# Loading the image with its channels on the partitions, one column at a time, in place of transposes on TensorE

## The chip, the cores and the metric

The kernel runs on one core of a Trainium2 chip. The metric is the device time of one execution in microseconds (us). The kernel before was run three times: median 3004.53 us, from 3003.02 to 3005.59. Everything read from a profile comes from one further execution, recorded by the hardware profiler.

Engine names are those of the profile: PE is TensorE (matmuls), PEld its weight loads, DVE is VectorE, ACT is ScalarE, POOL is GpSimd. SP only starts transfers and waits for events; SPq and ACTq stand for DMA issues on the queues of SP and ACT.

## The reference

The input x has the shape 4 x 64 x 64 x 64: four elements of the batch, each an image of 64 rows (h) by 64 columns (w) with 64 channels (c), in fp32. Four attention layers follow each other, and the elements do not depend on each other. Of the first layer, which the change feeds, the reference computes this:

```python
b, h, w, c = x.shape
n = h * w                                            # 4096 tokens
q = (einsum('bhwc,cf->bhwf', x, Wq) + bq).reshape(b, n, c)
k = (einsum('bhwc,cf->bhwf', x, Wk) + bk).reshape(b, n, c)
v = (einsum('bhwc,cf->bhwf', x, Wv) + bv).reshape(b, n, c)
attn = softmax(einsum('bic,bjc->bij', q, k), axis=-1)   # 4096 x 4096 per element
out = einsum('bmn,bmc->bnc', attn, v)
x = gamma * out.reshape(b, h, w, c) + x
```

The kernel calls the four layers layer0 to layer3. Layer1 is a smaller attention, of 4096 queries by 1024 pooled keys. Layer2 and layer3 are again full 4096 x 4096 attentions, each with a group normalisation in front. So three layers have 4096 x 4096 scores for each of the four elements, and these scores and the sums with v make up nearly all of the work.

## The kernel before, in words

**Layout.** Most of the time an element's image lies in SBUF as a tile xT of 128 partitions by 2048 fp32 values: the 64 channels of the left half of the image (columns 0 to 31) on partitions 0 to 63, those of the right half (columns 32 to 63) on partitions 64 to 127, and along a partition the tokens of that half in the order row, column (h times 32 plus w). The matmuls of all layers read this layout, since the channels are what they sum over. In memory the image has its channels innermost, so xT is the transpose of what a plain load gives.

**How xT comes about.** `load_x` (L645) starts eight transfers of 128 KB on the SP queue (L653) into a tile xin that has tokens on the partitions and runs of 64 channels, 256 bytes each, along them. `transposed` (L909) then makes two groups of eight transposes of 128 x 128 on TensorE (L916) into a PSUM tile, and copies each group to half of xT (`evacuate`, L858: on VectorE at L862 for element 1, on ScalarE at L870 for elements 2 and 3; for element 0 on both). `before0` (L919) calls it, then `project` (L874, matmuls at L883) for the queries q, then `swapped` (L889, two transfers on SP at L893, which exchange the halves of q), then `values` (L896, matmuls at L902).

**Steps.** The program is written in steps (`step`, L808). In a step of layer0 (L949), layer2 or layer3 (`attention`, L1184) two blocks of scores are made (128 x 1024; matmuls L971 or L1199, exponentials L975 or L1204), and two earlier blocks are multiplied with v (L996 or L1234). A phase is 64 steps, and there are twelve: layer0 of elements 0 and 1, layer2 of element 0, layer0 of element 2, layer2 of element 1, and so on. All other work is background: a chain of generators handed to `background` (L777), which is advanced one piece at a time inside the steps (`advance`, L798) at a tempo given for the phase. A piece ends at each `yield`. What is left of the chain at the end of a phase is emitted at once (`drain`, L786). A function can also be tied to the start of a given step through the dictionary `before` (L773).

The order in which this program emits instructions is the order on each engine. It does not tie the engines to each other: an engine waits only for the data and the buffers that its next instruction needs. The queue of SP takes its transfers in the order in which they were emitted.

**Where the load and the transposes stand.** In the first phase (steps 0 to 63, layer0 of element 0) the background at tempo 1 ends with: the constants of the later layers, the load of element 1 (emitted in step 28), six pauses, `before0` of element 1 (transposes in steps 35 and 36, `project` in steps 37 and 38, `values` in steps 39 and 40), and the load of element 2 (step 41). Element 2's transposes run in the third phase (layer2 of element 0). Element 3 is loaded at the end of the background of the fourth phase, and transposed in the fifth.

**Buffers.** xin, xT, q, k, v and other tiles of 128 x 2048 come from one pool of 13 buffers (L626, `x_tile`, L631). A tile takes a buffer when it is first written, and gives it back after its last use.

**Other transfers on SP.** Between the loads stand the exchanges of halves: q_swapped and k_swapped (L893) and pg (L1059, in layer1), and at the end the output. In the compiled program a transfer also waits for the one that stands eight transfers earlier, since eight completion counters are handed round.

Of the kernel before, what the change touches and what calls it, by code (L numbers as in the profile page):

```python
# [597 lines left out]
def fast_path(tc: tile.TileContext, a: dict, out: bass.AP, bad):  # L598
# [9 lines left out]
    nc = tc.nc  # L608
    x = a["x"]
    B, H, W, C = x.shape  # L610
    N = H * W
    P = 128
    W2 = W // 2
# [6 lines left out]
    MID, ALONE, LATE, END = range(4)  # L620
# [10 lines left out]
    x_tile = lambda name: x_p.tile([P, S], FP, tag="x", name=name)  # L631
    p_tile = lambda: p_p.tile([P, 1024], FP, tag="p", name="p")
    o_tile = lambda name: o_p.tile([P, 512], FP, tag=name, name=name)
    half = lambda i: slice(i * C, (i + 1) * C)
# [6 lines left out]
    def tokens(ap):  # L641

        return ap.rearrange("(k r) (i w) c -> r w k i c", r=4, i=2)

    def load_x(st, parts=((slice(None), lambda r, i: nc.sync.dma_start),)):  # L645
        if "xin" not in st:
            st["xin"] = x_tile("xin").rearrange("p (k i c) -> p k i c", i=2, c=C)
        t = st["xin"]
        src = tokens(x[st["b"]])
        for ks, queue in parts:  # L650
            for r in range(4):
                for i in range(2):
                    queue(r, i)(t[r * W2 : (r + 1) * W2, ks, i, :], src[r, :, ks, i, :])  # L653

    def ctile(shape, name):
        return const.tile(shape, FP, tag=name, name=name)
# [3 lines left out]
    def column(name, src, reps=2):  # L660
        t = ctile([P, 1], name)
        n = P // reps
        for i in range(reps):
            load[0](t[i * n : (i + 1) * n, :], src.rearrange("(c o) -> c o", o=1))
        return t
# [106 lines left out]
    now = [0]  # L772
    due, before, urgent = {}, {}, []  # L773
# [3 lines left out]
    def background(tempo, *phases):  # L777
        def pieces():
            for ph in phases:
                yield from ph  # L780

        assert back["at"] is None
        back.update(gen=pieces(), credit=0.0, tempo=tempo)
        back["at"] = next(back["gen"], None)
# [64 lines left out]
    def banks(on):  # L849

        if on == "both" and now[0] < 2:
            bank = [acc_tile(), acc_tile()]
            return bank, bank
        s = s_tile()
        bank = [s[:, chunk(i)] for i in range(2)]
        return bank if on == "both" else s, bank

    def evacuate(on, dst, src, bias=None):  # L858

        if on == "DVE":  # L860
            if bias is None:
                nc.vector.tensor_copy(dst, src)  # L862
            else:
                nc.vector.tensor_scalar(dst, src, bias, None, ALU.add)
        elif on == "both":
            m = dst.shape[-1] // 2
            evacuate("DVE", dst[:, 0:m], src[0], bias)
            evacuate("ACT", dst[:, m:], src[1], bias)
        elif bias is None:
            nc.scalar.copy(dst, src)  # L870
        else:
            nc.scalar.activation(dst, src, AF.Identity, bias=bias)
# [16 lines left out]
    def swapped(name, t):  # L889

        o = x_tile(name)
        for i in range(2):
            nc.sync.dma_start(o[half(i), :], t[half(1 - i), :])  # L893
        return o
# [14 lines left out]
    def transposed(on, st):  # L909
        xin = st.pop("xin")  # L910
        xT = st["x"] = x_tile("xT")
        for g in range(2):
            yield MID
            s, bank = banks(on)
            for i in range(8):
                nc.tensor.transpose(bank[i // 4][:, ds(i % 4 * P, P)], xin[:, g * 8 + i, :, :].rearrange("p i c -> p (i c)"), ident)  # L916
            evacuate(on, xT[:, wide(g)], s)

    def before0(on, st):  # L919
        yield from transposed(on, st)  # L920
        q = x_tile("q")
        yield from project(on, q, blocks[0][0], st["x"], blocks[0][1])
        st["q"] = q, swapped("q_swapped", q)
        st["v"] = x_tile("v").rearrange("p (j f) -> p j f", f=C)
        yield from values(st["v"], wv0, st["x"], bv0)
# [16 lines left out]
    def second_half(st, v):  # L942
        yield from values(v, wv0, st["x"], bv0)
        for g in st.pop("todo"):
            yield MID
            for _ in g:
                pass

    def layer0(st):  # L949

        q, k, v = st.pop("q"), st["x"], st.pop("v")
        pairs = NB * NC // 2
        acc, ps, zs, scaled = {}, {}, {}, {}
        zsum, rz = check_columns(NB)

        def queries(m, i, e):

            c, n = divmod(m // 2, 4)
            return q[(c + i) % 2][half(i), ds(c // 2 * 1024 + m % 2 * 512 + n * P + e * C, C)]

        def first(u):
            m, c = divmod(u, NC)
            if c == 0:
                zs[m] = small.tile([P, NC], FP, tag="z0", name="z0")
            s = s_tile()
            for i in range(2):
                for e in range(2):  # L970
                    nc.tensor.matmul(  # L971
                        s[half(e), chunk(i)], queries(m, i, e), k[half(i), chunk(c)], start=True, stop=True
                    )
            p = ps[u] = p_tile()
            nc.scalar.activation(p, s, AF.Exp, accum_out=zs[m][:, c : c + 1])  # L975
            if c == NC - 1:
                nc.vector.tensor_reduce(zsum[:, m : m + 1], zs.pop(m), AX.X, ALU.add)  # L977
                nc.vector.reciprocal(rz[:, m : m + 1], zsum[:, m : m + 1])

        def scale(t):  # L980
            vs = scaled[t] = z_p.tile([P, C], FP, tag="vs", name="vs", bufs=1)
            for e in range(2):
                if 0 <= t - e < pairs:
                    m = 2 * (t - e) // NC
                    nc.scalar.activation(  # L985
                        vs[half(e), :], v[half(e), m, :], AF.Copy, scale=rz[half(e), m : m + 1]
                    )

        def add(t, e, n, vs, cols):

            if 0 <= t < pairs:
                m, c = divmod(2 * t + n, NC)
                if m == 0 and e == 0 and c not in acc:
                    acc[c] = acc_tile()
                for i in range(2):
                    nc.tensor.matmul(  # L996
                        acc[c][half(i), cols], vs[half(e), :], ps[2 * t + n][half(e), chunk(i)][:, cols],
                        start=(m == 0 and e == 0), stop=(m == NB - 1 and e == 1),
                    )
                    yield  # L1000

        def adds(t, n, within=None):
            for cols in parts(within, t * 2 < NC or t >= pairs - NC // 2):
                lower, upper = add(t, 0, n, scaled[t], cols), add(t - 1, 1, n, scaled[t], cols)
                for row_tile in (lower, upper) * 3:
                    next(row_tile, None)
            if n == 1:
                del scaled[t]
                for u in (2 * t - 2, 2 * t - 1):
                    ps.pop(u, None)  # L1010

        def finish(cs):
            xT = st["x"]
            for c in cs:
                nc.vector.scalar_tensor_tensor(xT[:, chunk(c)], acc.pop(c), gamma0, xT[:, chunk(c)], ALU.mult, ALU.add)
            if not acc:
                st["done0"] = True

        start = now[0]
        for t in range(pairs + 1):  # L1020
            g = start + t + 3
            before.setdefault(g, []).append(lambda t=t: scale(t))
            due.setdefault(g, []).extend([lambda *within, t=t, n=n: adds(t, n, *within) for n in range(2)])
        for g, cs in ((2, (0, 1)), (3, (2, 3))):
            due[start + pairs + g].append(lambda cs=cs: finish(cs))
        for t in range(pairs):
            step(lambda: (first(2 * t), first(2 * t + 1)))
        return start + pairs + 4
# [483 lines left out]
    s0, s1, s2, s3 = state  # L1512
    def rest(phase):
        yield MID
        yield from phase
# [7 lines left out]
    st0 = transposed("both", s0)  # L1523
# [70 lines left out]
    for n, dsts in spectra:  # L1594
        w_d, u_d = a["L1_conv_w_" + n], a["L1_conv_u_" + n]
        r, d = w_d.shape
        w, u = scratch2[:, at : at + d], scratch2[:, at + d : at + 2 * d]
# [100 lines left out]
    def pause(n):  # L1698
        yield from [MID] * n

    def loads(st):
        yield MID
        load_x(st)


    background(1.0, rest(st0), second_half(s0, s0["v"]), pause(6), constants(), loads(s1), pause(6), before0("DVE", s1), loads(s2))
    layer0(s0)
    drain()
    background(3.0, layer1("DVE", s0, False), before2("DVE", s0))
    free = layer0(s1)  # L1710
    drain()
    background(3.0, layer1("ACT", s1, True), before0("ACT", s2))
    free = layer2(s0, free)
    drain()
    background(1.0, before2("DVE", s1), loads(s3))
    free = layer0(s2)
    drain()
    background(3.0, layer1("ACT", s2, True), before0("ACT", s3))
# [99 lines left out]
```

## Time and profile before

| What | Value |
|---|---|
| median of three runs | 3004.53 us (3003.02 to 3005.59) |
| the profiled execution's own time | 3005.78 us |
| its span, first to last instruction | 3003.7 us |
| granted TensorE clock, mean | 0.999 |
| PE busy | 2979.2 us |
| ACT busy | 1943.8 us |
| DVE busy | 1760.1 us |
| DMA queue of SP: packets, MB, share of 16 engines | 40080, 21.17 MB, 3.7% |
| transposes of elements 1 to 3 (L916) | 48, median 273 ns one by one |
| their evacuations on VectorE (L862) | 2 of 1.23 us |
| loads of x, 128 KB each: median from issue to landing | 5.0 us |

How to read it: the span is the profiled execution from its first to its last instruction; its own time has 2.1 us more around it. An engine's busy time is the time in which it executed something. Matmuls overlap each other, so eight transposes of 273 ns took 1.09 us together. A DMA packet is what one of the 16 DMA engines moves for one descriptor, a contiguous run of bytes; the share of 16 engines is the time that all packets took, over 16 times the stretch looked at. In the listings of groups and of the timeline, a line begins with its start and duration in us, then engine, source line, operation, output<-input, shapes and count.

### The profile page before, as it was taken

To read this page: it belongs to the slowest core of one execution; us is meant where nothing else is said; L and a number is where in the kernel's file an instruction comes from. 1 tells how busy PE (TensorE), PEld (TensorE's weight loads), DVE (VectorE), ACT (ScalarE), POOL (GpSimd) and SP (SyncE) were. 2 spreads that over 40 slices of the span, in tenths; PEclk is the share of its full clock that TensorE was granted. 3 is DMA by queue.
4 is the path that set the end of the run, shared out by engine and by line. 5 is a ranking of instruction groups with operands and counts; after the bars stand their busy time and mean duration, and the time that the engine had idled before them with its cause. 6 is when DMAs were issued, how large, how long until landed. Compare 5 with 4: busy or idle time off the path is not lost.

```text
span 3003.7 us, 64700 instructions
## 1 busy us (share of the span) xinstructions
PE 2979.2 (99%) x28509; PEld 1133.0 (38%) x28509; DVE 1760.1 (59%) x2003; ACT 1943.8 (65%) x2816; POOL 34.1 (1%) x32
## 2 busy tenths in 40 slices
PE   9999999999999999999999999999999999999998
PEld 4333233433444433344443333333343334333333
DVE  1211332587731068772017887777887777877777
ACT  6877778666588866557886655655555655555554
POOL 0000000000000000000000000000000000000000
PEclk9999999999999999999999999999999999999999
DMA  2010000000001000000000000000000000000000
GB/s 37 2 29 5 1 1 2 19 2 1 15 1 29 1 5 1 15 2 10 7 2 5 2 8 9 19 5 8 5 19 6 17 1 1 12 12 5 9 5 9
DMA packets 42081, 25.79 MB, mean 9 GB/s; under 512 B 39872, under 2 KB 39872, under 8 KB 40384
## 3 DMA queue, kind: packets, MB, share of 16 engines
q1 hardware_dynamic: 40080, 21.17, 3.7%
q8 instruction: 225, 3.69, 0.5%
q10 hardware_dynamic: 1712, 0.41, 0.1%
q14 instruction: 64, 0.52, 0.1%
HBM read 4.79 MB, written 4.19 MB: 3 GB/s over the span
## 4 chain that ended last, share of the span: by engine, by line
PE 98%; ACT 1%; SPq 0%; DVE 0%; issue 0%; DMA 0%; ACTq 0%; DVEq 0%
PE acc L1234 30%; PE s L1199 30%; PE acc L996 15%; PE s L971 14%; PE s L1079 2%; PE acc L1105 1%; ACT p L1085 1%; PE s L883 1%; PE s L1105 1%; PE s L1262 1%; PE s L1346 0%; PE s L902 0%; PE s L1260 0%; PE s L1443 0%; PE s L1366 0%; PE s L1051 0%
## 5 line engine op out<-in xcount | busy, mean ns | idle before, releaser
L1204 ACT ACTIVATE p<-s 128x1024 f32<-128x1024 f32 x1024 | 994.8, 1022 | 705.6 <-PE s L1199 694.0
L1210 DVE TENSOR_TENSOR zacc<-zacc,p 128x1024 f32<-128x1024 f32 x960 | 1174.1, 1223 | 372.2 <-ACT p L1204 334.4
L975 ACT ACTIVATE p<-s 128x1024 f32<-128x1024 f32 x512 | 519.9, 1016 | 42.7 <-PE s L971 24.3
L1234 PE MATMUL acc<-p,v 64*64 64x512 f32 (+1 forms) x4456 | 525.2, 558 | 0.0
L996 PE MATMUL acc<-p,vs 64*64 64x512 f32 (+1 forms) x4224 | 512.2, 578 | 0.5 <-ACT vs L985 0.5
L1199 PE MATMUL s<-q,k 64*64 64x512 f32 x2048 | 495.5, 593 | 2.1 <-ACT p L1085 2.1
L1234 PE MATMUL acc<-p,hT 64*64 64x512 f32 x4096 | 494.1, 590 | 0.0
L971 PE MATMUL s<-xT,q 64*64 64x512 f32 x2048 | 487.4, 591 | 2.5 <-DVE v L903 0.6
L971 PE MATMUL s<-xT,q_swapped 64*64 64x512 f32 x2048 | 488.4, 591 | 0.0
L1199 PE MATMUL s<-q,xT 64*64 64x512 f32 x2048 | 486.9, 589 | 0.0
L1199 PE MATMUL s<-q,h_swapped 64*64 64x512 f32 x2048 | 479.4, 589 | 0.0
L1199 PE MATMUL s<-q,k_swapped 64*64 64x512 f32 x2048 | 477.6, 593 | 0.0
L977 DVE TENSOR_REDUCE all_z<-z 128x1 f32<-128x4 f32 x128 | 20.1, 157 | 643.2 <-ACT p L975 643.2
L1234 PEld LDWEIGHTS acc<-p,v 64*64 64x64 f32 x4456 | 179.9, 133 | 285.0 <-issue 280.0
L996 PEld LDWEIGHTS acc<-p,vs 64*64 64x64 f32 x4224 | 176.3, 133 | 270.3 <-issue 206.5
L985 ACT ACTIVATE vs<-v,all_r 64x64 f32<-64x64 f32 x512 | 177.2, 346 | 145.2 <-PE acc L996 72.4
L1234 PEld LDWEIGHTS acc<-p,hT 64*64 64x64 f32 x4096 | 156.7, 133 | 263.8 <-issue 263.1
L971 PEld LDWEIGHTS s<-xT,q_swapped 64*64 64x64 f32 x2048 | 145.8, 133 | 146.3 <-issue 114.2
L1199 PEld LDWEIGHTS s<-q,h_swapped 64*64 64x64 f32 x2048 | 143.9, 133 | 141.2 <-issue 135.5
L971 PEld LDWEIGHTS s<-xT,q 64*64 64x64 f32 x2048 | 145.8, 133 | 134.1 <-issue 106.0
L1199 PEld LDWEIGHTS s<-q,xT 64*64 64x64 f32 x2048 | 143.4, 133 | 140.1 <-issue 137.7
L1199 PEld LDWEIGHTS s<-q,k 64*64 64x64 f32 x2048 | 140.1, 132 | 148.3 <-issue 100.2
(233 smaller groups left out, 1560.2 us busy)
## 6 DMA issues: line engine op xcount, KB each, us to landing
k_swapped<-k SPq DMA_DIRECT2D x8, 512.0 KB, 6.0
h_swapped<-xT SPq DMA_DIRECT2D x8, 512.0 KB, 5.3
out_dram<-turned SPq DMA_DIRECT2D x62, 64.0 KB, 1.9
xin<-in_x_dram SPq DMA_DIRECT2D x24, 128.0 KB, 5.0
q_swapped<-q SPq DMA_DIRECT2D x6, 512.0 KB, 5.4
pg<-pg SPq DMA_DIRECT2D x8, 128.0 KB, 2.3
xin<-in_x_dram SPq DMA_DIRECT2D x12, 64.0 KB, 2.3
xin<-in_x_dram ACTq DMA_DIRECT2D x4, 64.0 KB, 2.6
```

The source lines that it names most:

```text
L883: nc.tensor.matmul(bank[i][half(e), :], w[half(i), half(e)], rhs[half(i), chunk(2 * j + (1 - e if exchanged else e))], start=True, stop=True,)
L971: nc.tensor.matmul(s[half(e), chunk(i)], queries(m, i, e), k[half(i), chunk(c)], start=True, stop=True)
L975: nc.scalar.activation(p, s, AF.Exp, accum_out=zs[m][:, c : c + 1])
L985: nc.scalar.activation(vs[half(e), :], v[half(e), m, :], AF.Copy, scale=rz[half(e), m : m + 1])
L996: nc.tensor.matmul(acc[c][half(i), cols], vs[half(e), :], ps[2 * t + n][half(e), chunk(i)][:, cols], start=(m == 0 and e == 0), stop=(m == ...
L1079: nc.tensor.matmul(ss[e][half(m), chunk(i)], pgs[0 if e == d else 1][r, ds(n * P + m * C, C)], th[r, chunk(2 * j + i)], start=True, stop=True,
L1085: nc.scalar.activation(pk[e], ss[e], AF.Exp)
L1105: nc.tensor.matmul(acc[quarter(q), :], g[:, k, :], ps[j, k][q // 2][:, chunk(q % 2)], start=(k == 0 or not bank), stop=(k == NK - 1 or not ...
L1199: nc.tensor.matmul(s[half(e), chunk(i)], k[(j + i) % 2][half(i), ds(j // 2 * P + e * C, C)], q[half(i), chunk(c)], start=True, stop=True,)
L1204: nc.scalar.activation(p, s, AF.Exp)
L1210: add = lambda: nc.vector.tensor_tensor(zaccs[c], p0, p, ALU.add)
L1234: nc.tensor.matmul(accs[c][e][half(i), cols], v[half(e), j, :], p[half(e), chunk(i)][:, cols], start=(j == 0), stop=(j == NB - 1),)
```

## The change

Elements 1, 2 and 3 are no longer loaded into xin and transposed. A new function, `load_transposed`, writes xT straight from memory: for each of the 64 image columns (half i, column w within the half) one transfer on SP, whose destination is 64 partitions (channels) by 64 rows with a step of 32 values, and whose source is the same elements in memory, where neighbouring channels are 4 bytes apart and neighbouring rows 16 KB. Neither side has a run of more than one fp32 value along its last dimension, so each transfer is made of 4096 descriptors of 4 bytes. Element 0 keeps the load and the transposes.

The 64 transfers of an element are tied to the starts of steps: for element 1 two in each step from step 6 of the first phase on, for elements 2 and 3 one in each step of the second and of the fourth phase. `before0` takes the finished tile and begins with `project`. In the first phase the chain loses the two loads and has fourteen pauses between the constants and `before0`. The generator `loads` goes away.

```diff
+    def load_transposed(st, first, rate):
+
+        xT = st["x"] = []
+        src = x[st["b"]].rearrange("h (i w) c -> i w c h", i=2)
+
+        def column(n):
+            if n == 0:
+                xT.append(x_tile("xT"))
+            i, w = divmod(n, W2)
+            dst = xT[0][half(i), :].rearrange("c (h w) -> w c h", w=W2)
+            nc.sync.dma_start(dst[w], src[i, w])
+
+        for n in range(W):
+            before.setdefault(now[0] + first + n // rate, []).append(lambda n=n: column(n))
+
     def before0(on, st):
-        yield from transposed(on, st)
+        (st["x"],) = st["x"]
         q = x_tile("q")
...
-    def loads(st):
-        yield MID
-        load_x(st)
-
-
-    background(1.0, rest(st0), second_half(s0, s0["v"]), pause(6), constants(), loads(s1), pause(6), before0("DVE", s1), loads(s2))
+
+    background(1.0, rest(st0), second_half(s0, s0["v"]), pause(6), constants(), pause(14), before0("DVE", s1))
+    load_transposed(s1, 6, 2)
     layer0(s0)
     drain()
     background(3.0, layer1("DVE", s0, False), before2("DVE", s0))
+    load_transposed(s2, 0, 1)
     free = layer0(s1)
     drain()
     background(3.0, layer1("ACT", s1, True), before0("ACT", s2))
     free = layer2(s0, free)
     drain()
-    background(1.0, before2("DVE", s1), loads(s3))
+    background(1.0, before2("DVE", s1))
+    load_transposed(s3, 0, 1)
     free = layer0(s2)
```

## The prediction

> **What bounds the kernel.** I read the page's busy line first, then the chain that ended last.
>
> ```profile
> span 3003.7 us, 64700 instructions
> ...
> PE 2979.2 (99%) x28509; PEld 1133.0 (38%) x28509; DVE 1760.1 (59%) x2003; ACT 1943.8 (65%) x2816; POOL 34.1 (1%) x32
> ...
> PE 98%; ACT 1%; SPq 0%; DVE 0%; issue 0%; DMA 0%; ACTq 0%; DVEq 0%
> ```
>
> TensorE is busy 99% of the span and is 98% of the chain: work taken off it shortens the kernel, and any wait put in front of it lengthens the kernel by the whole wait, because nothing later has slack to take it back.
>
> The timeline of ScalarE in the stage that holds the second element's transposes shows the pitch of a step (each step begins with an exp of L975):
>
> ```profile
> 142.01 1.02 ACT L975 ACTIVATE p<-s 128x1024 f32<-128x1024 f32 x1
> ...
> 145.44 1.02 ACT L975 ACTIVATE p<-s 128x1024 f32<-128x1024 f32 x1
> ...
> 150.06 1.02 ACT L975 ACTIVATE p<-s 128x1024 f32<-128x1024 f32 x1
> ...
> 154.68 1.02 ACT L975 ACTIVATE p<-s 128x1024 f32<-128x1024 f32 x1
> ```
>
> A plain step is 145.44 - 142.01 = 3.43 us. The two steps with eight transposes each are 4.62 us. TensorE's timeline of the same stretch says what was inserted, and when the first reader of xT came:
>
> ```profile
> 147.03 1.09 PE L916 MATMUL s<-ident,xin 128*128 128x128 f32 x8
> ...
> 151.64 1.09 PE L916 MATMUL s<-ident,xin 128*128 128x128 f32 x8
> ...
> 156.15 1.04 PE L883 MATMUL s<-xT,A 64*64 64x512 f32 x8
> ```
>
> SP's timeline shows when its queue is free and what it waits at; SP runs ahead of the step in which an instruction was written:
>
> ```profile
> 40.67 5.50 SPq L653 DMA_DIRECT2D xin<-in_x_dram  x8
> 162.86 1.13 SPq L893 DMA_DIRECT2D q_swapped<-q  x2
> 164.44 7.67 SPq L653 DMA_DIRECT2D xin<-in_x_dram  x8
> 289.69 1.11 SPq L1059 DMA_DIRECT2D pg<-pg  x2
> 526.84 1.10 SPq L893 DMA_DIRECT2D k_swapped<-k  x2
> ```
>
> Element 1 is loaded at 40.67, behind the last weights, though its load stands in step 28 (near 121 us). Element 2 is loaded right behind q_swapped.
>
> The DMA view of two windows prices packets: 12.9 to 14.9 us, where small bias columns of 4-byte elements move alone, then 43.5 to 46.5 us, where 256-byte rows of x saturate the engines:
>
> ```profile
> DMA packets 336, 0.00 MB, mean 1 GB/s; under 512 B 336, under 2 KB 336, under 8 KB 336
> q1 hardware_dynamic: 336, 0.00, 8.0%
> ```
>
> ```profile
> DMA packets 2111, 0.52 MB, mean 175 GB/s; under 512 B 2111, under 2 KB 2111, under 8 KB 2111
> q1 hardware_dynamic: 2111, 0.52, 130.9%
> ```
>
> A 4-byte packet takes 8.0% x 16 engines x 2.0 us / 336 = 7.6 ns with the engines nearly idle. Saturated, an engine gets through a 256-byte packet every 16 x 3.0 us / 2111 = 22.7 ns. The same count in a quiet window (28 to 33 us: 650 packets, 12.1%) is 12.1% x 16 x 5 us / 650 = 14.9 ns, so saturation costs 1.52 times.
>
> **What the Trainium skill says.** "DMA: Bandwidth & Descriptors", Rules for kernel authors: a strided last dimension becomes one descriptor per element; the trace agrees for the bias columns (336 packets, 0.00 MB). The same page, Why small descriptors are slow: each packet carries a fixed cost of about 3 cycles whatever its size. The trace fits: 4 bytes cost half of 256 bytes (7.6 against 14.9 ns), not a sixty-fourth. The same page, Specifications: transfers under 512 B are read, modified and written; no run here separates that. "TensorE: Matmul & The Clock Gate", What's actually happening: after an idle window of about 3.4 us TensorE runs at half clock for a similar time; here the first sixteen L883 matmuls took 3.47 us against 2 x 1.04 later.
>
> **Removed: 48 transposes.** Two steps in each of three elements become plain: 6 x (4.62 - 3.43) = 6 x 1.19 = 7.1 us off TensorE. The pairs of elements 2 and 3 agree (734.98 and 739.59: 4.61 apart). The evacuations removed with them (two of 1.23 us on VectorE, four of 1.01 us on ScalarE) lie beside TensorE in steps where both engines idle, and are worth nothing more; if that cover were gone the ScalarE ones would cost 4.0 us in all.
>
> **Added: 3 x 64 transfers on SP.** A column is 64 channels x 64 rows = 4096 descriptors, 256 for each of 16 engines and one closing packet: 257. An element is 64 x 257 = 16,448 packets per engine, so each nanosecond per packet costs 16.4 us. Issue is not the limit: SP spent 0.43 to 0.5 us on a transfer in its free stretches, 64 of which are about 32 us. That a transfer of 4096 descriptors issues as fast is not shown. Cost per packet, unknown, from both sides:
> - 7.6 ns, quiet: 1.95 us a column, 125 us an element. Below this only if packets overlap on an engine, as the 130.9% allows (at 0.76 of it, 5.8 ns, 95 us).
> - 11.6 ns, 7.6 with the factor 1.52 of the 256-byte stream: 2.98 us a column, 191 us.
> - If descriptors come no faster than the most that the trace shows (253 GB/s in the best slice of the saturated window, 0.99 packets per ns in all): 4.14 us, 265 us.
>
> I take the middle of the first two, 9.6 ns: 2.47 us a column, 158 us an element. At full stream I expect the quiet price to grow somewhat, but less than for packets that also carry 256 bytes.
>
> **Element 1, start and deadline.** The columns stand behind the weights, in one of the six buffers of thirteen that no earlier tile has used, so they start where the x load starts now, 40.7 us, whatever step they are written in. The last lands at 40.7 + 2.1 (the landing time of a small weight) + the stream: 42.8 + 158 = 200.7. The first reader, L883, moves. Its step is now the 37th; with fourteen pauses in place of the load's own seven, and no transposes, it is the 42nd. Step 34 began at 142.01, eight plain steps add 27.5, and L883 comes 1.47 into its step (156.15 - 154.68): 171.0. Every column writes all rows, so the first matmul needs all 64. TensorE, in order, stands from 171.0 to 200.7: 29.7 us, plus half of a 3.4 us cold stretch, 1.7. Queued behind L883 on TensorE are all scores and sums of the first layer; ScalarE and VectorE wait for those. What is late next is q_swapped and everything after, by the same amount.
>
> The stall starts at (171.0 - 42.8) / 16.448 = 7.79 ns a packet, barely over the quiet price.
>
> **Elements 2 and 3.** SP runs ahead here too. For element 2 a few columns go behind q_swapped, most behind pg at 289.7, the last few behind k_swapped at 526.8; L883 reads them at 744.1. Some 54 columns fit between pg and k_swapped up to (526.8 - 290.8) / 54 = 4.4 us each. Element 3 has about 23 columns at 751, the rest behind k_swapped at 913; pg at 1089.8 gives those 41 columns 4.3 us each. At 2.47 us nothing waits: cost 0, hidden by the layer that runs meanwhile. Past 4.4 us k_swapped is late, which has only 8.7 us from landing (532.8) to its reader (541.5). The loads of xin that go away cost nothing now.
>
> **Sum.** 29.7 + 1.7 - 7.1 = +24.3 us. Against the profiled execution (span 3003.7, 3005.8 with what lies around it) that is 3028.0 of span, 3030.1 in all; the median of the runs shown is 1.3 us lower, 3004.5, so 3028.8.
>
> **Rivals.**
> - *Not slower.* Packets stream at the quiet price or below; the decisive point is 7.79 ns. The last column lands before 171 and only the removal is left: 3004.5 - 7.1 = 2997.4. For it: 7.6 is measured, and packets overlap. Against it: that price is from engines 8% busy, and 256-byte packets got 1.52 times dearer.
> - *A tie.* Between 7.8 and 8.5 ns the stall, up to 11.4 us, lies within the 0.2% (6 us) that a measurement of this kernel can tell from no change.
> - *Descriptor supply.* At 4.14 us a column the stall is 42.8 + 265 - 171 = 137 us: 3004.5 + 137 + 1.7 - 7.1 = 3136. For it: 0.99 packets per ns is the best seen. Against it: those packets carried 256 bytes, so the bytes may have set that rate.
> - *A buffer wait.* Element 3's tile is taken some 26 steps earlier, when ten of thirteen are in use and the normalisation needs two: just enough. If one is missing, SP waits and k_swapped is late. I give this no separate chance.
>
> That the transposes were free cannot be: TensorE is busy through those steps.
>
> **Chances.** Stall of 11 to 91 us (8.5 to 13.3 ns): 0.43, likeliest, own range 3010 to 3090. Not slower: 0.36. Tie: 0.09. Above 13.3 ns, descriptor supply included: 0.12. Faster by over 0.2% is 0.36, within 0.2% is 0.09, slower is 0.55. The range runs from the not-slower case, 2996, to the end of the likeliest, 3090, and leaves out the 0.12 above and little below.
>
> **What would show it.** No L916 matmuls after 17 us; six plain steps of 3.43. In the DMA view from 41 us on, the packets of 64 columns: their count over time gives the price, 9.6 ns an engine if I am right. On TensorE, one wait of about 30 us ahead of L883 near 171 us, released by a DMA into xT, and none ahead of L883 in elements 2 and 3. I am wrong if that wait is missing (price below 7.8), or far longer, or if k_swapped or pg is late, which means that the queue backs up where I gave it room.

## The result, and the profile after

| Kernel | Median | Runs |
|---|---|---|
| before | 3004.91 us (3003.02 to 3005.59) | 4 |
| changed | 3195.32 us (3193.89 to 3195.94) | 4 |

The ratio is 1.0633, with a 95% interval from 1.0621 to 1.0646. The forecast was slower, 3028.8 us in a range of 2996 to 3090; the direction was right, the size was not. The profiled span grew from 3003.7 to 3194.2 us, by 190.5 us.

The page of the changed kernel has the same lines as those shown of before:

```profile
span 3194.2 us, 64773 instructions
...
PE 2981.9 (93%) x28461; PEld 1137.3 (36%) x28461; DVE 1757.4 (55%) x2001; ACT 1938.7 (61%) x2812; POOL 34.0 (1%) x32
...
PE 81%; SPq 16%; ACT 1%; DMA 1%; issue 0%; DVE 0%; ACTq 0%; DVEq 0%
```

TensorE does as much as before (2981.9 us against 2979.2, part of it at a slower clock: the mean granted clock was 0.969 against 0.999), but in a longer span. In the chain that ended last, SP's queue now holds 16%: the transfers of the columns have become part of the path. Behind the new function the lines of the changed kernel stand 15 further down: its L1074 is L1059 of before. SP's timeline says where the path was held:

```profile
40.34 298.20 SPq L929 DMA_DIRECT2D xT<-in_x_dram  x64
...
464.65 240.56 SPq L929 DMA_DIRECT2D xT<-in_x_dram  x51
705.32 4.97 SPq L893 DMA_DIRECT2D k_swapped<-k  x2
...
1088.03 189.57 SPq L929 DMA_DIRECT2D xT<-in_x_dram  x40
1277.69 5.74 SPq L1074 DMA_DIRECT2D pg<-pg  x2
```

Element 1's 64 columns start where the rows started before (40.34), and hold SP for 298.20 / 64 = 4.66 us each on average. k_swapped and the pg of element 2 follow directly on a run of columns: they had to wait for it. TensorE's timeline has the waits; the bracket at the end of a line is the idle time before it and what ended it:

```profile
194.91 1.97 PE L883 MATMUL s<-xT,A 64*64 64x512 f32 x4 [23.56 <-DMA xT<-in_x_dram]
...
345.66 1.12 PE L883 MATMUL s<-xT,A 64*64 64x512 f32 x2 [148.78 <-DMA xT<-in_x_dram]
...
1286.04 2.00 PE L1094 MATMUL s<-th,pg 8*64 8x512 f32 x12 [14.73 <-DMA pg<-pg]
```

L883 arrives at 171.35 and waits twice, for the left half of the image and for the right, 172.3 us in all. Near 1286 the scores of layer1 (L1094) wait 14.73 us for the late pg. Between 716 and 718 k_swapped is 1.3 us late.

The DMA view from 60 to 160 us, in which SP issued nothing but columns:

```profile
DMA packets 87194, 0.49 MB, mean 5 GB/s; under 512 B 87184, under 2 KB 87184, under 8 KB 87184
q1 hardware_dynamic: 87184, 0.35, 47.6%
```

A packet takes 47.6% x 16 x 100 us / 87,194 = 8.7 ns of an engine, but an engine gets one through only every 16 x 100 us / 87,194 = 18.4 ns. The engines are idle for half of the time, while SP is held at every transfer. This gap became the subject of the experiments.

Where the 190.5 us went, by setting the first exponential of each step side by side in the two profiles (ScalarE's timelines):

| Place | Change in us |
|---|---|
| element 1: 172.3 of waiting, -2.4 for two plain steps, the rest (3.9, by difference) TensorE's slow start after the wait and what refills behind it | +173.8 |
| layer2 of element 0: k_swapped late | +2.4 |
| element 2: transposes gone | -2.4 |
| layer1 of element 2: pg late (14.7 of waiting and what follows it) | +19.0 |
| element 3: transposes gone | -2.4 |
| the rest, by difference | +0.1 |

The slow start is seen at L883: its matmuls took 1.1 us at 345.66, 0.59 in the plain stretches. Element 2's row is read so: the steps around its former transposes lasted from 733.44 to 762.37 us before, and from 909.57 to 936.12 in the changed kernel, 28.93 against 26.55.

### The profile page after: what moved, and what is told of

The parts are those of the page before. It is cut to its first block, busy times and chain, and to the rows that moved or that the text cites. A ratio compares the mean times of both kernels' runs of the same rounds, so it can differ in the third digit from the quotient of the medians.

```text
span 3194.2 us, 64773 instructions
## 1 busy us (share of the span) xinstructions
PE 2981.9 (93%) x28461; PEld 1137.3 (36%) x28461; DVE 1757.4 (55%) x2001; ACT 1938.7 (61%) x2812; POOL 34.0 (1%) x32
## 4 chain that ended last, share of the span: by engine, by line
PE 81%; SPq 16%; ACT 1%; DMA 1%; issue 0%; DVE 0%; ACTq 0%; DVEq 0%
PE acc L1249 27%; PE s L1214 27%; SPq L929 15%; PE s L986 9%; PE acc L1011 9%; PE s L1094 2%; PE acc L1120 1%; ACT p L1100 1%; PE s L883 1%; PE s L1120 1%; PE s L1277 1%; PE s L1361 0%; PE s L902 0%; DMA xT<-in_x_dram 0%; PE s L1275 0%
```

## The experiments

All times of the kernel before in these runs lie between 3003.07 and 3006.08 us. Where a ratio is given, the kernel ran 4 to 21 times; the others ran once, with differences far larger than that spread. The theories to be told apart were four: descriptors come at one rate from what generates them (*supply*, a rival of the prediction, with 4.14 us a column); each transfer has a *fixed price*; the *source addresses* hold the reads up; the *scattered writes* into SBUF do.

**Does the wait for element 1 account for the loss?** `a_elem1_transposed` gives element 1 its row load and transposes back:

```diff
-    background(1.0, rest(st0), ..., constants(), pause(14), before0("DVE", s1))
-    load_transposed(s1, 6, 2)
+    background(1.0, rest(st0), ..., constants(), loads(s1), pause(6), before0("DVE", s1, True))
```

(`loads` is back, and with `True` `before0` begins with `transposed`.)

> Element 1 goes back to the row load and the transposes; elements 2 and 3 keep their columns. If the lost time is the wait for element 1's columns (172 us of waits at L883 in the changed kernel) plus the late pg of element 2 (14.7 us of wait, about 19 us of steps), the first goes and the second stays: 3004.9 - 3.5 (transposes of elements 2 and 3) + 19 to 24 = about 3020 to 3026 us. If the small packets slow the other engines by contention wherever they run, more than 3040.

Measured: 3021.04 us, ratio 1.0059 (1.0042 to 1.0076). The late pg is what remains, beside 0.9 us for k_swapped, in its list of waits:

```profile
PE s L1097 <- DMA pg<-pg: 14.2, 1, 14.2
```

So nearly all of the loss is waiting at two places, and no loss by the 4-byte packets running beside the other work is seen. That the wait is landing minus reader was tried from the other side: `m_late_reader` is the changed kernel with `pause(28)` for `pause(14)`.

> The changed kernel with its columns, only the first reader of element 1 14 steps later (28 pauses for 14). The wait at L883 should shrink by what the reader moved, 14 x 3.43 = 48 us: 172 to 124 us, 3195 to 3147 us. If the load starts or runs with the steps instead of ahead of them, the time stays near 3195 us.

Measured: 3148.57 us. TensorE's timeline:

```profile
346.25 1.12 PE L883 MATMUL s<-xT,A 64*64 64x512 f32 x2 [126.02 <-DMA xT<-in_x_dram]
```

The reader moved by 48.9 us (171.35 to 220.23), the landing did not (345.66, 346.25), and the wait shrank from 172.3 to 126.0. SP does run ahead of the steps.

**What sets 4.66 us a column?** First the number of transfers and the two access patterns. `e_halves` cuts each column by rows, `d_rows` walks the source along the channels, `d2_dst` writes neighbouring values:

```diff
 e_halves:
-            nc.sync.dma_start(dst[w], src[i, w])
+            for rows in (slice(0, H // 2), slice(H // 2, H)):
+                nc.sync.dma_start(dst[w][:, rows], src[i, w][:, rows])
 d_rows:
-        src = x[st["b"]].rearrange("h (i w) c -> i w c h", i=2)
+        src = x[st["b"]].rearrange("h (i w) c -> i w h c", i=2)
 d2_dst:
-            dst = xT[0][half(i), :].rearrange("c (h w) -> w c h", w=W2)
+            dst = xT[0][half(i), :].rearrange("c (w h) -> w c h", w=W2)
```

> Every column is cut into two transfers of 32 rows, so twice as many transfers with half as many descriptors each. If the cost goes with descriptors (about 1.14 ns each), a transfer takes 2.3 us on SP, element 1 lands near 345 us as in the changed kernel, and the time stays near 3195 us. If 4.7 us is a price per transfer, element 1 lands near 645 us and the time is about 3500 us or more.

> The same 4096 four-byte descriptors per transfer and the same destination, but the source is walked so that an engine's neighbouring descriptors are neighbouring values in memory (the values of row and channel change places, so the output is another one). If descriptors come at one rate from their generator, 4.7 us a transfer and about 3195 us as before. If reads at a step of 16 KB are what is slow, clearly less: 2 to 3 us a transfer, 3030 to 3090 us.

> The same 4096 four-byte reads per transfer, but written to neighbouring values of each partition instead of with a step of 128 bytes (the tokens lie in another order, so the output is another one). Descriptor supply: unchanged, 4.7 us a transfer and about 3195 us. If scattered small writes into SBUF are what is slow, clearly less.

Measured: 3504.05, 3413.45 and 3192.14 us. SP's timelines, in the same order:

```profile
40.55 423.51 SPq L930 DMA_DIRECT2D xT<-in_x_dram  x128
...
40.74 387.30 SPq L929 DMA_DIRECT2D xT<-in_x_dram  x64
...
40.44 298.99 SPq L929 DMA_DIRECT2D xT<-in_x_dram  x64
```

`d2_dst` excludes the step of the writes. `d_rows` has the same number of descriptors and transfers and is 1.30 times slower, so neither a fixed supply nor a fixed price can be the whole; but it went against the address theory as I had put it too, which expected neighbouring values to be read faster. The total of `e_halves` agrees with the number for a price per transfer, but only by chance: its load ended at 464 us, between the two landings that were expected, and the rest of its loss is 199.2 us of waits for k_swapped and pg, which that number did not contain. Its 3.31 us for 2048 descriptors could come from a fixed 2 us and 0.66 ns a descriptor, or from the fact that a transfer now reaches 32 rows of memory instead of 64.

The next three runs separate these. `h_chan` cuts each column by channels, which keeps all 64 rows in every transfer. `j_diag` is the column itself with rows 16.25 KB apart instead of 16 KB. `g_rows` takes an image row per transfer, whose tokens lie 256 bytes apart:

```diff
 h_chan:
-            nc.sync.dma_start(dst[w], src[i, w])
+            for cs in (slice(0, C // 2), slice(C // 2, C)):
+                nc.sync.dma_start(dst[w][cs, :], src[i, w][cs, :])
 j_diag:
-        src = x[st["b"]].rearrange("h (i w) c -> i w c h", i=2)
+        flat = x.rearrange("b h w c -> (b h w c)")
...
-            nc.sync.dma_start(dst[w], src[i, w])
+            at = (st["b"] - 1) * N * C + i * W2 * C + w * C
+            src = flat[at : at + H * (W + 1) * C].rearrange("(h q) -> h q", h=H)[:, 0:C].rearrange("h c -> c h")
+            nc.sync.dma_start(dst[w], src)
 g_rows:
-        src = x[st["b"]].rearrange("h (i w) c -> i w c h", i=2)
+        src = x[st["b"]].rearrange("(i h) w c -> i h c w", i=2)
...
-            dst = xT[0][half(i), :].rearrange("c (h w) -> w c h", w=W2)
+            dst = xT[0][half(i), :].rearrange("c (h w) -> h c w", w=W)
```

> Every column in two transfers of 32 channels and all 64 rows, so the same places of memory as in the changed kernel with half of the descriptors in each transfer. The cut by rows took 3.3 us a transfer. If that came from reaching half of the rows' places only, this cut keeps all of them: about 2.4 us a transfer and about 3195 us. If a transfer has a fixed part (4.7 and 3.3 us would give 1.9 us plus 0.68 ns a descriptor), 3.3 us again and about 3500 us.

> Sixty-four transfers of 4096 four-byte descriptors as in the changed kernel, into the same places, but the rows of a column lie 16.25 KB apart in memory instead of 16 KB (one image column further with each row, so the output is another one). If the pace is set by how many places of the memory the 64 rows of a column fall on, a step that is not a power of two spreads them and a transfer takes 2 to 3.5 us instead of 4.7: 3020 to 3120 us. If it is set by the descriptors or by a fixed price per transfer, nothing changes: 4.7 us and about 3195 us.

> Again 64 transfers of 4096 four-byte descriptors, but one transfer takes a whole image row, whose 64 tokens lie 256 bytes apart in 16 KB of memory (the two halves of xT then hold upper and lower rows instead of left and right columns, so the output is another one). Memory places: fastest of all, near the engines' own 7 to 9 ns a packet, 1.8 to 2.5 us a transfer, element 1 lands at 160 to 205 us, total 3000 to 3035 us. Descriptor supply or a fixed price: 4.7 us and about 3195 us.

Measured: 3192.10 (`h_chan`), 3047.00 (`j_diag`) and 3035.23 us (`g_rows`). SP's timeline and the DMA view from 50 to 100 us of `j_diag`:

```profile
40.55 173.05 SPq L931 DMA_DIRECT2D xT<-in_x_dram  x64
```

```profile
DMA packets 73248, 0.37 MB, mean 7 GB/s; under 512 B 73242, under 2 KB 73242, under 8 KB 73242
q1 hardware_dynamic: 73242, 0.29, 82.4%
```

The same transfers, packets and destinations, with 256 bytes added to the step between rows: 2.70 us a column instead of 4.66. The engines are 82.4% busy instead of 47.6%, and a packet itself takes as long as before (82.4% x 16 x 50 us / 73,248 = 9.0 ns). With the load faster, k_swapped and pg are no longer late, and one wait of 46.2 us at L883 is left. The kernel reads for each element the memory of the one before it, but the place isn't the cause: its load of element 2 took 2.71 us a column (51 in 138.03 us), from the memory whose columns took 4.66 in the changed kernel. The load of `g_rows` and that of `h_chan`:

```profile
40.30 164.31 SPq L929 DMA_DIRECT2D xT<-in_x_dram  x64
...
40.06 300.11 SPq L930 DMA_DIRECT2D xT<-in_x_dram  x128
```

`g_rows` took 2.57 us a transfer, just above the 2.5 that was expected at most. `h_chan` settles the other question: halving the transfers without changing the rows that they reach leaves 300.1 us. There is no fixed price to be seen at this size.

All of element 1's loads, from SP's timelines:

| Kernel | Distance of the tokens in memory | Tokens in a transfer | Transfers | us in all | ns per descriptor |
|---|---|---|---|---|---|
| changed | 16 KB | 64 | 64 | 298.2 | 1.14 |
| `d2_dst` | 16 KB, writes adjacent | 64 | 64 | 299.0 | 1.14 |
| `h_chan` | 16 KB | 64 | 128 | 300.1 | 1.14 |
| `e_halves` | 16 KB | 32 | 128 | 423.5 | 1.62 |
| `d_rows` | 16 KB, channels in turn | 64 | 64 | 387.3 | 1.48 |
| `j_diag` | 16.25 KB | 64 | 64 | 173.1 | 0.66 |
| `g_rows` | 256 B | 64 | 64 | 164.3 | 0.63 |
| `g2_rows_half` | 256 B | 32 | 128 | 191.0 | 0.73 |

**A version that is faster than both.** By rows the layout of the reference is had with one transfer for each row and half. `g2_rows_half` only changes this; `k_rows_late` and `n_rows_later` also move the first reader of element 1 back; `o_rows23` leaves element 1 to the transposes and takes elements 2 and 3 by rows:

```diff
 g2_rows_half:
-        src = x[st["b"]].rearrange("h (i w) c -> i w c h", i=2)
+        src = x[st["b"]].rearrange("h (i w) c -> i h c w", i=2)
...
-            dst = xT[0][half(i), :].rearrange("c (h w) -> w c h", w=W2)
-            nc.sync.dma_start(dst[w], src[i, w])
+            dst = xT[0][half(i), :].rearrange("c (h w) -> h c w", w=W2)
+            for r in (2 * w, 2 * w + 1):
+                nc.sync.dma_start(dst[r], src[i, r])
 k_rows_late, n_rows_later (28 and 32):
-    ... constants(), pause(14), before0("DVE", s1))
+    ... constants(), pause(28), before0("DVE", s1))
```

> The reference's own layout by image rows: one transfer for each row and half, 128 transfers an element of 2048 descriptors whose 32 tokens lie 256 bytes apart. If the step of 16 KB was what cost, near 1.3 us a transfer, element 1 lands at 205 to 215 us, one wait of 35 to 45 us at L883 is left and no late pg or k_swapped: 3030 to 3045 us. If half a row reaches too few places (as half a column did), 1.7 us or more, above 3080 us.

> By rows as in the kernel beside it, and with 28 pauses in place of 14, so that the first reader of element 1 comes 14 steps (48 us) later, near 219 us, after its last row has landed. If the wait is only landing minus reader, nothing waits, and what is left is the removal of the transposes: 3004.9 - 5 to 7 = 2998 to 3000 us. If the small packets cost something else on the path, it shows here: above 3003 us.

> By rows, with 32 pauses: the reader comes 4 steps (13.7 us) after that of the kernel with 28 pauses, which still waited 12.2 us. If landing minus reader is all that was left, no wait at L883 remains and the time is 3004.9 - 5 to 7 = 2998 to 3000 us, below the kernel before. If queries and values are now too late for the next phase, a new wait of some us appears at the start of layer0 of element 1, and the time is near 3005 us.

> Element 1 by transposes as before, elements 2 and 3 by rows, which have slack to land. Four groups of eight transposes are gone, about 0.9 us each by the steps of the changed kernel: 3004.9 - 3.5 = about 3001.5 us, and no wait for x, pg or k_swapped. If the small packets cost the other engines something, nothing is left of it: 3004 us or more.

Measured: `g2_rows_half` 3061.59 us, above its number: 1.49 us a transfer instead of 1.3, and three waits at L883 of 55.4 us in all.

```profile
40.38 190.99 SPq L930 DMA_DIRECT2D xT<-in_x_dram  x128
```

`k_rows_late` 3015.64 us, ratio 1.0033 (1.0021 to 1.0045), a miss: the rows landed later than I had put it, and one wait was left. Its 12.2 us account for most of the 16 to 18 us by which the time lies above the expected 2998 to 3000.

```profile
238.13 1.08 PE L883 MATMUL s<-xT,A 64*64 64x512 f32 x1 [12.20 <-DMA xT<-in_x_dram]
```

`n_rows_later` 3001.37 us, ratio 0.9988 (0.9981 to 0.9995), 1.4 us above what was expected of it, and `o_rows23` 3001.37 us, ratio 0.9987 (0.9981 to 0.9994). The page of `n_rows_later`:

```profile
span 3000.0 us, 65025 instructions
...
PE 2975.7 (99%) x28461; PEld 1135.9 (38%) x28461; DVE 1757.3 (59%) x2001; ACT 1939.2 (65%) x2812; POOL 34.1 (1%) x32
```

TensorE is at 99% again and no L883 waits for a transfer. By their medians over 21 runs both are about 4 us (0.13%) faster than the kernel before, so little that it takes that many runs to tell. The transposes of element 1 add nothing to that: `n_rows_later` gains 2.4 us up to its late reader, and has 0.4 left of it at the end of the phase, because `project` costs 2.0 and 1.6 us in the steps at which it now stands against 0.9 and 0.9 at its old place. For elements 2 and 3 it gains 1.8 and 1.6 us, less than the 2.4 each of the changed kernel, because there too `project` is dearer by rows. Its trace has a likely reason: at L883 stand 60 semaphore instructions of 51 ns in front of TensorE's weight loads, against 25 in the changed kernel and 7 before, and eight of its matmuls take 1.40 us (at 734.51) for 1.07 in the changed kernel (at 910.96). By rows the 512 tokens of a matmul come from 16 transfers, which may be why it waits for more events; no run tests this apart. The 0.9 us a group in the expectation of `o_rows23` is not what the changed kernel's steps show (1.2), so that it came true owes something to this cost.

## Why the prediction was wrong

**Where TensorE would wait: right.** L883 arrived at 171.35 (forecast 171.0), element 1's stream started at 40.34 (40.7), and SP ran ahead of the steps. The kernel with the later reader shows that the wait is landing minus reader. In one detail the working was off: the first matmuls need one half of the image only, so the wait came in two parts, of the same sum.

**The price of a column: the step that failed.** The prediction took "the middle of the first two, 9.6 ns", 2.47 us a column. Measured were 18.4 ns, 4.66 us of SP's time and, by the landing, (345.66 - 42.8) / 64 = 4.73 us a column. Both of the estimates in that middle are prices of a packet on its engine. That price was nearly right: 8.7 ns by the packet's own time, and 16 x 50 us / 73,248 = 10.9 ns as the pace of a stream in `j_diag`; that 9.6 lies between them is partly luck, since the factor 1.52 sets a pace (22.7 ns) against a packet's own time (14.9 ns). What was left out is a limit that the packet's own time does not contain, in where the reads go: with rows 16 KB apart a column took 4.66 us, with rows 16.25 KB apart 2.70. This term was mis-sized, and with it the stall (172.3 us for 29.7).

The range ended at 91 us of stall. The rival of descriptor supply came nearest with 4.14 us and 3136 us, but for the wrong reason: the same descriptors came 1.7 times faster in `j_diag`. A hint was at hand: the Trainium skill, "DMA: Bandwidth & Descriptors", Latency and other measured facts, tells of copies between tensors in HBM that slow down when the distance of their rows is a large power of two (from nearly full speed at 512 KiB to half at 4 MiB), and that 4 KiB of padding restored it while 192 bytes did not. The runs here show a slowdown at 16 KB for 4-byte reads, where 256 bytes more were enough; whether it is the same effect is not shown.

**"Issue is not the limit".** SP was held 4.66 us at each transfer where I had counted 0.43 to 0.5. In `j_diag` it was held 2.70 us for the same transfers, and in the changed kernel a column with no other column before it held SP for 0.66 us (at 40.34) or 1.88 us (at 354.97 and 710.33). So most of the 4.66 is the queue backing up behind the reads, not the price of issuing.

**Elements 2 and 3: the thresholds held, the price crossed them.** 4.4 and 4.3 us a column had been named as the points from which k_swapped and pg are late. At 4.7 us both were: pg cost 19.0 us of steps, k_swapped 2.4. At 2.70 us (`j_diag`) neither was late. The shares were 24 and 40 columns for 23 and 41.

**The removal: right.** 7.1 us were forecast, and the steps of the changed kernel gave 2.37 + 2.38 + 2.35 = 7.1. The kernels by rows keep about 4 of it, since their `project` is dearer. The slow start after the wait was taken as 1.7 and came to 3.9 us together with what refills behind it.

**The buffer wait** given no chance did not appear. The rival "not slower" fell by the price: with rows in place of columns and a later reader it is what `n_rows_later` does.

What stays open: which part of the memory path the 16 KB step overloads, and how the addresses are mapped. The runs show that the pace follows the distance and the order of the source addresses, and not the step of the writes or the number of transfers at a given set of rows. They do not show that a power of two is the reason: one other large step was tried, and 256 bytes, a power of two as well, was fastest. `e_halves` reaches fewer rows (1.62 against 1.14 ns), but also writes half as many values along each partition; the same halving at 256 bytes cost less (0.73 against 0.63 ns), and no run parts the two. Nor is it shown what sets the 2.57 to 2.70 us that remain: in `j_diag` the engines were busy for 82.4% of the time, not all of it, so a supply of descriptors at about 0.63 ns each is not excluded there.

## What to carry to other kernels

Price a stream of small descriptors by its pace and not by the time of one packet, and look at the distance of the source addresses: here the reads of a column lay 16 KB apart, and 256 bytes more made the same transfers 1.7 times faster. If the same data can be cut along another dimension, as by rows here, try that first. When a load moves onto a queue that also carries small urgent transfers, work out for each stretch between them how many of its transfers fit; here that sum named both later stalls.

## What the runs showed of the hardware that was not expected

- Rows 16 KB apart against 16.25 KB, read in 4-byte pieces: 4.66 against 2.70 us for 4096 descriptors.
- The time that the profile gives a packet did not contain this hold-up: 8.7 ns at 47.6% busy, 9.0 ns at 82.4%. Half-idle engines behind a queue that held SP at every transfer were its sign.
- The destination's step did not matter here: 298.2 us for the load with written values 128 bytes apart, 299.0 us with neighbouring ones.
- The order of the reads mattered too: the same 64 rows of 64 values took 6.05 us a transfer when each partition took the 64 neighbouring values of one row (`d_rows`), and 4.66 us when it took one channel of all 64 rows, 16 KB apart.
